# Two multiplication levels for items 0 and 1 too, with the weights' quarters formed in item 0 and the last convolution's banks named by number

## The chip, the core and the metric

The kernel runs on one core of a Trainium2 chip. The core has a matrix engine (TensorE, PE in the profile), a vector engine (VectorE, DVE), an activation engine (ScalarE, ACT), a general engine (GpSimd, POOL) and a queue engine that only issues transfers (SyncE, SP). Every engine runs its own instructions in the order in which they were written, and waits on others through semaphores. The metric is the device time of one whole execution in microseconds.

## The reference

Thirty-two items of 512 nodes and 512 features, in fp32, go through a masked attention layer with 8 heads of 64, a residual and a layer norm, and then through a graph convolution, a residual and a second layer norm:

```
q, k, v = x @ Wq + bq, x @ Wk + bk, x @ Wv + bv           # (32, 512, 512) each, split into 8 heads of 64
scores  = q k^T / 8 + where(adj == 0, -1e9, 0)            # (32, 8, 512, 512)
y       = softmax(scores) v
x1      = layernorm(x + y)
norm_adj = adj * rsqrt(deg)[:, None] * rsqrt(deg)[None, :],   deg = adj.sum(axis=1)
out     = layernorm(x1 + norm_adj @ (x1 @ W1) + b1)
```

`adj` is one 512x512 matrix for all items.

## The kernel before

**Projections by fewer products.** A 512x512x512 product (keys, queries, values, or the convolution's second factor) is cut into 2x2 blocks of 256 and computed with seven block products in place of eight; the price is sums and differences of blocks beforehand. The four such sums of a weight are `weigh_part` (line 228), those of `x` are `combine` (174). In one level each of the seven products (the table `CHAIN`, or `PLAIN_FIRST`, line 349, for item 0, whose operands come in another order) is four 128x256 matmuls. In two levels four of the eight matmul groups are taken into quarters: `LEAF` (367) is seven steps of four 128x128 matmuls on 128-wide quarters, and `OUTER` (368) three further products of the first level, four 128x256 matmuls each. Two levels need quarters of the operands too: `quarter` (179) forms those of `x` and `weigh_quarter` (272) those of a weight, both on POOL. A tile of a weight therefore has ten slots: four blocks, three sums, three of quarters. The fourth quarter sum goes back into one of the blocks, so that a weight with all four quarters can no longer be used in one level.

`seven` (374) walks such a table: a step multiplies into a PSUM bank of its region (A, B, D, M), and then `put` copies the bank to SBUF on ACT or `add` adds it on DVE. Where the next step accumulates into the same bank, or a later region takes over its number, PE has to wait until `put` or `add` has read it. `bank` hands out the eight PSUM banks in turn, or by `at=`.

Before, items 0 and 1 run in one level: `keys_and_queries` (458) makes a pair of key and query heads at once, and `values_of` (396) takes `PLAIN_FIRST` and `CHAIN`. From item 2 on `keys_or_queries` (481) and the second half of `values_of` run in two levels.

**The order of the work.** A loop over items (from about line 990) is laid out by hand. Item b does: scores and values products of head pairs 0 and 2 (`stretch`, 608, with `scores`, 535), the keys and queries of item b+1, scores and values products of pairs 1 and 3, then the convolution of item b-1 mixed with the values of item b+1. `play(main, beside)` writes the PE steps of `main` one by one, and after step n the work of the other engines given under key n in `beside`. Nothing is reordered after that: an engine meets its instructions exactly in this order, so a DVE instruction written ahead of another one delays it even if it is not urgent.

The work beside PE that the change touches:

- `accumulate` (552): POOL adds up the numerators `e` of a head pair over four node blocks into `acc`; `fold` (623): DVE turns and reduces `acc` to `folded`; `inverse_all` (684): PE spreads `folded` with one matmul, DVE takes the maximum with a tiny number and the reciprocal; `scale_head` (722): ACT scales one node block of one head with it (32 of these for an item).
- `turn` (143): DVE transposes an item's `x` in 32x32 blocks, two instructions an item. `turn_first` (151) does it for item 0's with PE.
- `adjacency` (314): PE transposes `adj` in 16 blocks, DVE makes the mask from the bank, ACT copies it twice. `degrees` (329) is a DVE reduction of 128x2048 and a few small operations; `compare` (323) is a DVE comparison and a DVE reduction over 128x512, done four times, for a flag that selects the general kernel if the inputs are out of the ordinary.
- `swap` (280): `Wq`'s and `Wv`'s sums share one tile, `wqv`, and are loaded into it in turn from DRAM, where they are stored (`stored`) in item 0.
- `load_residual` (198): four loads of an item's `x` rows, and a gather that adds the bias row.
- `block` (807): the convolution of the last item, in four PSUM banks; `extend`: POOL additions of the last but one.

In item 0 (from line 959) the values come first, then the weights' sums, then keys and queries for head pairs by twos with the adjacency beside them. In the loop's pass b = 0 the keys and queries of item 1 are computed with `fold`, `degrees`, `compare` and the sums of `W1` beside them, and the values of item 1 with folds, turns and the fourth quarters of `Wv` beside them.

Of the kernel before, what the change touches and what calls it, by code (L numbers as in the profile page):

```python
# [10 lines left out]
F32 = mybir.dt.float32  # L11
# [4 lines left out]
ALU = mybir.AluOpType  # L16
# [34 lines left out]
def unshifted(  # L51
# [57 lines left out]
    def run(pieces):  # L109
        for f in pieces:  # L110
            f()
# [67 lines left out]
    def quarter(at):  # L179
        old, new = XT[:, 1:5].rearrange("p k u (t o) -> p k u t o", t=2), QUARTERS  # L180
        to, a, c = (
            (new[:, 0], old[:, :, 0, 1], old[:, :, 0, 0]), (new[:, 1], old[:, :, 1, 1], new[:, 0]),
            (new[:, 2], old[:, :, 1, 1], old[:, :, 0, 1]), (old[:, :, 0, 1], old[:, :, 1, 0], new[:, 1]),
        )[at]
        gpsimd.tensor_tensor(to, a, c, ALU.subtract)
# [62 lines left out]
    wv = NUM[:, :4].rearrange("p e k (u o) -> p (e k) u o", u=2)  # L248
# [18 lines left out]
    wk_quarters, wqv_quarters = quarters_in(wk), quarters_in(wqv)  # L267
# [4 lines left out]
    def weigh_quarter(w, new, at, engine, last=None):  # L272
# [3 lines left out]
            (new[:, 2], old[:, :, 0, 0], old[:, :, 0, 1], ALU.subtract), (old[:, :, 0, 1] if last is None else last, old[:, :, 1, 0], new[:, 1], ALU.subtract),  # L276
        )[at]
        engine.tensor_tensor(to, a, c, op)

    def swap(k, slots=10):  # L280
        sync.dma_start(wqv[:, :slots], stored[k][:, :slots])
# [32 lines left out]
    def adjacency(k):  # L314
        for m in (2 * k, 2 * k + 1):
            p = bank([P, N])
# [79 lines left out]
    def values_of(b):  # L396
# [21 lines left out]
        if b < 2:  # L418
            return seven(CHAIN if b else PLAIN_FIRST, multiply, put, add)
# [37 lines left out]

    def keys_and_queries(b, r):
        def multiply(p, i, j, fresh):
            for c, w in enumerate((wk, wqv)):  # L460
                for u in range(2):
                    tensor.matmul(
                        p[:, c, :], w[:, i, u, ts(r, P)], XT[:, j, u, :],
                        start=fresh and c == 0 and u == 0, stop=u == 1, skip_group_check=True,
                    )

        def out(i, j):
            begin_kq(b)
            return KQ[b, r + 2 * i][:, :, ts(j, HALF)]

        def put(q, p):
            g = r + 2 * q[0]
            for c in range(2):
                scalar.activation(out(*q)[:, c], p[:, c], AF.Identity, bias=bias[:, c, g : g + 1], scale=1.0)

        def add(q, p):
            vector.tensor_add(out(*q), out(*q), p)

        return seven(CHAIN if b else PLAIN_FIRST, multiply, put, add)

    def keys_or_queries(b, c):
# [45 lines left out]
        inner, outer = (({"A": 2, "D": 3, "B": 0}, {"A": 4}), ({"A": 5, "D": 3, "B": 0}, {"A": 2}))[c]  # L527
        leaf = seven(LEAF, multiply_quarters, put, add, (4, P), places=inner)
        return leaf, [spread_last], seven(OUTER, multiply, None, add_outer, places=outer)

# [265 lines left out]
    def convolve(b):  # L796
# [10 lines left out]
        def block(m):  # L807
            if m == 0:
                t["p"] = [bank([P, N]) for _ in range(DT)]
# [157 lines left out]
    run(v[1:5])  # L967
    scalar.activation(wqv[:, :4], wqv[:, :4], AF.Copy, scale=SCALE)
    weigh(wk, gpsimd)
    run(v[5:])  # L970
    biases()
    wq_parts = each(lambda k: weigh_part(wqv, vector, k), *range(4))
    kq = keys_and_queries(0, 0)
    run(wq_parts[:2] + kq[:1] + wq_parts[2:3] + kq[1:2] + wq_parts[3:] + kq[2:])
    gather(first_rows, rows(bv))
    for w, new in ((wqv, wqv_quarters), (wk, wk_quarters)):
        for at in range(3):
            weigh_quarter(w, new, at, gpsimd)
    nc.sync.dma_start(stored[1][:, :7], NUM[:, :4].rearrange("p e k (u o) -> p (e k) u o", u=2)[:, :7])
    nc.sync.dma_start(stored[0], wqv)  # L980
    play(keys_and_queries(0, 1), {
        1: [lambda: adjacency(0)], 3: [lambda: turn(1, 0), lambda: adjacency(1)], 5: [lambda: turn(1, 1)],
    })
    for k in range(4):
        combine(1, k)
# [4 lines left out]
    for b in range(B):  # L990
# [31 lines left out]
        if b < LAST:  # L1022
            if b == 0:
                k0, k1 = keys_and_queries(1, 0), keys_and_queries(1, 1)
                main = [p for pair in zip(k0, k1) for p in pair]
                ahead_x = acts.tile([P, 2, 2, N], F32, name="x2", tag="lo", bufs=1)
                for j in range(2):
# [4 lines left out]
                    1: fold0, 2: [degrees], 3: weights[:1], 4: fold1, 5: weights[1:2] + exact[:1], 6: exact[1:2],  # L1032
                    7: weights[2:3], 8: exact[2:3], 9: weights[3:], 10: exact[3:],
                    12: each(lambda k: weigh_quarter(w1, w1_quarters, k, gpsimd), *range(3)),
                }
            else:
                (k_leaf, k_spread, k_outer), (q_leaf, q_spread, q_outer) = (keys_or_queries(b + 1, i) for i in range(2))
                main = (
                    k_leaf[:6] + k_outer[:1] + k_leaf[6:] + k_outer[1:2] + q_leaf[:6] + q_outer[:1] + q_leaf[6:]
                    + q_outer[1:2] + k_outer[2:3] + q_outer[2:3] + k_outer[3:] + q_outer[3:]  # L1040
                )
# [6 lines left out]
                    1: root + checks[:1], 2: checks[1:3], 3: checks[3:], 4: more[:1] if b > 1 else [],  # L1048
# [22 lines left out]
        elif b < LAST:  # L1071
            swap(1)
# [373 lines left out]
```

## Time and profile before

| What | Value |
| --- | --- |
| median of 3 timed runs | 2690.14 us (2690.1 to 2690.21) |
| the profiled execution's own time | 2690.48 us |
| span in its profile | 2688.5 us |
| PE busy | 2661.7 us (99%) |
| POOL, DVE, ACT busy | 2218.5 (83%), 2083.5 (77%), 1501.3 (56%) us |
| mean granted TensorE clock | 0.997 |
| keys and queries of item 0 / 1 / 3 | 22.70 to 48.72 / 63.00 to 87.37 / 23.22 us long |
| values of item 1 | 101.46 to 113.97 |
| convolution and values in a later item | about 31.0 us |

The profile names instructions by engine, operation and tile, `out<-in`; `xT` is the turned `x` with its block sums, `wk` and `wqv` the weights, `mm` a PSUM bank of a projection or of the convolution, `sc` one of scores, `av` one of values products, `kq` keys and queries, `e` the numerators. A fp32 matmul mostly leaves two records. All instructions show the line of one helper, L45, so they are told apart by tile. In a row of the timeline the first number is the start in microseconds, the second the length; a bracket at the end gives idle time before it and what ended it.

### The profile page before, as it was taken

To read this page: it belongs to the slowest core of one execution; us is meant where nothing else is said; L and a number is where in the kernel's file an instruction comes from. 1 tells how busy PE (TensorE), PEld (TensorE's weight loads), DVE (VectorE), ACT (ScalarE), POOL (GpSimd) and SP (SyncE) were. 2 spreads that over 40 slices of the span, in tenths; PEclk is the share of its full clock that TensorE was granted. 3 is DMA by queue.
4 is the path that set the end of the run, shared out by engine and by line. 5 is a ranking of instruction groups with operands and counts; after the bars stand their busy time and mean duration, and the time that the engine had idled before them with its cause. 6 is when DMAs were issued, how large, how long until landed. Compare 5 with 4: busy or idle time off the path is not lost.

```text
span 2688.5 us, 42635 instructions
## 1 busy us (share of the span) xinstructions
PE 2661.7 (99%) x15396; PEld 1935.9 (72%) x15396; DVE 2083.5 (77%) x3043; ACT 1501.3 (56%) x2677; POOL 2218.5 (83%) x1690
## 2 busy tenths in 40 slices
PE   9999999999999999999999999999999999999997
PEld 7677676776776866767767777677677677776765
DVE  4778877778778787787887787877878877778777
ACT  4456555565555565555655555555556555565554
POOL 5788888888898888888888888888888888888865
PEclk9999999999999999999999999999999999999999
DMA  6445446545455454455454554544555546545541
GB/s 196 148 109 160 137 115 165 150 124 144 132 149 150 125 155 142 119 156 142 142 140 119 166 149 119 156 137 131 153 129 158 138 117 166 153 118 148 148 97 53
DMA packets 422683, 373.30 MB, mean 139 GB/s; under 512 B 279872, under 2 KB 348992, under 8 KB 414272
## 3 DMA queue, kind: packets, MB, share of 16 engines
q1 hardware_dynamic: 388720, 304.16, 34.5%
q0 software_dynamic: 32736, 65.02, 15.7%
q8 instruction: 124, 2.03, 0.3%
q10 hardware_dynamic: 1008, 1.31, 0.1%
q14 instruction: 95, 0.78, 0.1%
HBM read 295.96 MB, written 41.16 MB: 125 GB/s over the span
## 4 chain that ended last, share of the span: by engine, by line
PE 96%; DVE 2%; POOL 1%; DMA 0%; ACT 0%; issue 0%; SPq 0%; POOLq 0%; DVEq 0%; ACTq 0%
PE mm L45 63%; PE sc L45 17%; PE av L45 16%; POOL acc L45 1%; DMA yT<-yb 0%; DVE st L45 0%; ACT yT L45 0%; DVE e L45 0%; SPq L45 0%; DVE folded L45 0%; DVE yT L45 0%; DMA xr<-in_x_dram 0%; DVE wk L45 0%; DVE yb L45 0%; DVE kq L45 0%
## 5 line engine op out<-in xcount | busy, mean ns | idle before, releaser
L45 POOL TENSOR_TENSOR acc<-acc,e 128x1024 f32<-128x1024 f32 x244 | 595.4, 2440 | 14.5
L45 DVE SCALAR_TENSOR_TENSOR e<-sc,maskT 128x1024 f32<-128x1024 f32 x512 | 585.2, 1216 | 21.3 <-PE sc L45 21.3
L45 ACT ACTIVATE e<-e 128x1024 f32<-128x1024 f32 x512 | 540.1, 1057 | 85.7 <-DVE e L45 55.4
L45 PE MATMUL sc<-kq 64*128 64x512 f32 x2048 | 456.9, 596 | 0.0
L45 PE MATMUL av<-e,v 128*64 128x512 f32 x2048 | 453.6, 595 | 0.3
L45 PE MATMUL mm<-xT,wk 128*128 128x256 f32 (+1 forms) x2512 | 393.3, 312 | 0.3 <-DVE kq L45 0.3
L45 POOL TENSOR_TENSOR xT<-xT 128x512 f32<-128x512 f32 x246 | 326.9, 1335 | 76.0 <-DVE xT L45 41.8
L45 PE MATMUL mm<-xT,wqv 128*128 128x256 f32 (+1 forms) x2512 | 387.9, 310 | 0.0
L45 PEld LDWEIGHTS mm<-xT,wk 128*128 128x128 f32 x2512 | 347.5, 191 | 46.7 <-DVE st L45 23.5
L45 PE MATMUL mm<-wqv,xT 128*128 128x128 f32 (+1 forms) x2456 | 379.0, 310 | 0.2 <-DVE v L45 0.2
L45 PEld LDWEIGHTS mm<-xT,wqv 128*128 128x128 f32 x2512 | 349.7, 191 | 21.3
L45 PEld LDWEIGHTS av<-e,v 128*64 128x64 f32 x2048 | 147.7, 137 | 298.9 <-issue 231.3
L45 POOL TENSOR_TENSOR e<-e 128x512 f32<-128x512 f32 x240 | 305.1, 1282 | 69.6 <-ACT e L45 54.5
L45 PEld LDWEIGHTS sc<-kq 64*128 64x128 f32 x2048 | 192.5, 187 | 232.5 <-issue 176.7
L45 PEld LDWEIGHTS mm<-wqv,xT 128*128 128x128 f32 x2456 | 343.7, 193 | 21.9 <-issue 0.8
L45 POOL TENSOR_TENSOR acc<-e 128x1024 f32<-128x1024 f32 x124 | 293.7, 2369 | 34.4 <-ACT e L45 34.4
L45 PE MATMUL mm<-w,e 128*128 128x128 f32 (+1 forms) x1680 | 297.9, 324 | 0.0
L45 ACT COPY kq<-mm 128x512 f32<-128x512 f32 x240 | 140.1, 584 | 256.2 <-PE mm L45 255.7
L45 PEld LDWEIGHTS mm<-w,e 128*128 128x128 f32 x1680 | 253.6, 191 | 24.8 <-DVE y L45 7.1
L45 DVE TENSOR_TENSOR v<-v,mm 128x512 f32<-128x512 f32 x217 | 146.2, 686 | 149.7 <-ACT v L45 76.3
L45 DVE SCALAR_TENSOR_TENSOR kq<-mm,bias,kq 128x256 f32<-128x256 f32 x420 | 183.7, 478 | 87.2 <-PE mm L45 49.8
L45 ACT ACTIVATE yT<-yT,inv 128x64 f32<-128x64 f32 x992 | 246.6, 337 | 0.0
(155 smaller groups left out, 3520.7 us busy)
## 6 DMA issues: line engine op xcount, KB each, us to landing
wqv<-wq_parts SPq DMA_DIRECT2D x30, 2560.0 KB, 11.7
wqv<-wv_parts SPq DMA_DIRECT2D x30, 2560.0 KB, 13.7
yT<-yb SPq DMA_DIRECT2D x508, 64.0 KB, 2.4
xr<-in_L_gnn_bv_dram POOLq DMA_DIRECT2D x31, 1024.0 KB, 11.2
xr<-in_x_dram SPq DMA_DIRECT2D x122, 256.0 KB, 4.2
e<-in_x_dram SPq DMA_DIRECT2D x240, 128.0 KB, 2.8
yT<-in_L_gnn_bias_dram POOLq DMA_DIRECT2D x30, 1024.0 KB, 16.5
out_dram<-y SPq DMA_DIRECT2D x116, 256.0 KB, 2.2
```

Source lines behind the costliest of these rows:

```text
L45: return self.tc.keep_in_program_order(op(*args, **kwargs))
```

## The change

Items 0 and 1 take two levels as well (item 0's values stay in one). `keys_and_queries` is gone; `projections` lists the steps of keys and queries in the order that item 2's had, and item 0 uses banks that differ in the leaf steps and in the regions of the outer ones. All four quarters of `Wk`, `Wv` and `Wq` are formed on POOL in item 0, and `Wv` and `Wq` are stored whole, so `swap` loads all ten slots each time and the patches of single slots in items 0 and 1 go. The quarters of item 0's `x` are formed on DVE. `adjacency` has its banks by number (6 and 7). In the pass b = 0 the four `compare` move from the keys and queries to the values of item 1, and behind them in DVE's order stand both `turn`s; the inverse of item 0 comes after the fifth leaf step. In the pass b = 1 the inverse comes two steps earlier, as in all later items, with the head scalings spread as there. In item 30 the residual load moves from step 8 to step 0 of the keys and queries. The last convolution's four banks are 0, 1, 3 and 5, and its tail does one addition fewer before its copies.

```diff
-    def quarter(at):
+    def quarter(at, engine=gpsimd):
...
-        gpsimd.tensor_tensor(to, a, c, ALU.subtract)
+        engine.tensor_tensor(to, a, c, ALU.subtract)
...
-    wv = NUM[:, :4].rearrange("p e k (u o) -> p (e k) u o", u=2)
+    wv = NUM[:, :5].rearrange("p e k (u o) -> p (e k) u o", u=2)
...
+    def weigh_quarters(w, new):
+        for at in range(4):
+            weigh_quarter(w, new, at)
+
+    def swap(k):
+        sync.dma_start(wqv, stored[k])
...
     def adjacency(k):
         for m in (2 * k, 2 * k + 1):
-            p = bank([P, N])
+            p = bank([P, N], at=6 + m % 2)
...
-        if b < 2:
-            return seven(CHAIN if b else PLAIN_FIRST, multiply, put, add)
+        if b == 0:
+            return seven(PLAIN_FIRST, multiply, put, add)
...
-        inner, outer = (({"A": 2, "D": 3, "B": 0}, {"A": 4}), ({"A": 5, "D": 3, "B": 0}, {"A": 2}))[c]
+        inner, outer = (
+            (({"A": 2, "D": 3, "B": 0}, {"A": 4}), ({"A": 5, "D": 3, "B": 0}, {"A": 2})) if b
+            else (({"A": 1, "D": 3, "B": 5}, {"A": 4}), ({"A": 0, "D": 3, "B": 5}, {"A": 2}))
+        )[c]
...
+    def projections(b):
+        (k_leaf, k_spread, k_outer), (q_leaf, q_spread, q_outer) = (keys_or_queries(b, c) for c in range(2))
+        main = (
+            k_leaf[:6] + k_outer[:1] + k_leaf[6:] + k_outer[1:2] + q_leaf[:6] + q_outer[:1] + q_leaf[6:]
+            + q_outer[1:2] + k_outer[2:3] + q_outer[2:3] + k_outer[3:] + q_outer[3:]
+        )
+        return main, k_spread, q_spread
...
-                t["p"] = [bank([P, N]) for _ in range(DT)]
+                t["p"] = [bank([P, N], at=k) for k in (0, 1, 3, 5)]
+                psum["n"] += 4
...
+    for k in range(3):
+        quarter(k, vector)
     scalar.activation(wqv[:, :4], wqv[:, :4], AF.Copy, scale=SCALE)
     weigh(wk, gpsimd)
+    weigh_quarters(wk, wk_quarters)
     run(v[5:])
+    quarter(3, vector)
     biases()
+    weigh_quarters(wv, wv_quarters)
+    nc.sync.dma_start(stored[1], wv)
     wq_parts = each(lambda k: weigh_part(wqv, vector, k), *range(4))
-    kq = keys_and_queries(0, 0)
...
-    for w, new in ((wqv, wqv_quarters), (wk, wk_quarters)):
-        for at in range(3):
-            weigh_quarter(w, new, at, gpsimd)
...
-    play(keys_and_queries(0, 1), {
-        1: [lambda: adjacency(0)], 3: [lambda: turn(1, 0), lambda: adjacency(1)], 5: [lambda: turn(1, 1)],
+    main, k_spread, q_spread = projections(0)
+
+    def store_parts():
+        weigh_quarters(wqv, wqv_quarters)
+        nc.sync.dma_start(stored[0], wqv)
+
+    play(main, {
+        0: wq_parts[:1], 1: wq_parts[1:2], 2: wq_parts[2:3], 3: wq_parts[3:] + [store_parts], 5: [lambda: adjacency(0)],
+        8: k_spread + [lambda: gather(first_rows, rows(bv))], 11: [lambda: adjacency(1)], 16: q_spread + [lambda: turn(1, 1)],
+        17: [lambda: turn(1, 0)], 18: [lambda: combine(1, 0)], 19: [lambda: combine(1, 1)],
     })
-    for k in range(4):
-        combine(1, k)
+    combine(1, 2)
+    combine(1, 3)
+    quarters()
...
             if b == 0:
-                k0, k1 = keys_and_queries(1, 0), keys_and_queries(1, 1)
-                main = [p for pair in zip(k0, k1) for p in pair]
...
-                    1: fold0, 2: [degrees], 3: weights[:1], 4: fold1, 5: weights[1:2] + exact[:1], 6: exact[1:2],
-                    7: weights[2:3], 8: exact[2:3], 9: weights[3:], 10: exact[3:],
-                    12: each(lambda k: weigh_quarter(w1, w1_quarters, k, gpsimd), *range(3)),
+                    2: fold0, 3: [degrees], 8: k_spread, 9: fold1 + weights[:2], 11: weights[2:], 16: q_spread,
+                    18: each(lambda k: weigh_quarter(w1, w1_quarters, k), *range(3)),
...
-                    5: first[:1] + ahead["root"] + store[:1], 6: store[1:3], 7: store[3:], 8: k_spread + load,
+                    0: load, 1: root + checks[:1], 2: checks[1:3], 3: checks[3:], 4: more[:1] if b > 1 else [],
+                    5: first[:1] + ahead["root"] + store[:1], 6: store[1:3], 7: store[3:], 8: k_spread,
...
-        if b == 0:
-            weigh_quarter(wqv, wqv_quarters, 3, gpsimd)
-            sync.dma_start(stored[0][:, 1:5, 0, P:], wqv[:, 1:5, 0, P:])
-            swap(1, 7)
-        elif b < LAST:
+        if b < LAST:
             swap(1)
...
-                play(values_of(1), {
-                    0: fold0, 1: fold1 + [weigh_values], 4: turn0, 5: end["inverse"],
-                    6: turn1 + combined + end["scale_heads"][24:] + end["scale_heads"][:8] + [lambda: swap(0)],
+                leaf, spread_last, outer = values_of(1)
+                heads = end["scale_heads"]
+                play(leaf[:6] + outer[:1] + leaf[6:] + [spread_last] + outer[1:], {
+                    0: fold0, 1: fold1 + [lambda: weigh_quarter(w1, w1_quarters, 3)], 4: end["inverse"],
+                    5: exact[:2] + heads[24:], 6: exact[2:] + heads[:8], 8: turn1 + turn0, 9: combined[:1], 10: combined[1:2],
+                    11: combined[2:] + [lambda: swap(0)],
                 })
...
-                        5: (end["inverse"] if b > 1 else []) + [lambda b=b: biased.extend(load_residual(b))],
-                        7: heads[:14] if b > 1 else end["inverse"], 11: heads[14:23] if b > 1 else heads[:23], 13: conv["open"] + ahead["judge"], 16: turn0,
+                        5: end["inverse"] + [lambda b=b: biased.extend(load_residual(b))], 7: heads[:14], 11: heads[14:23], 13: conv["open"] + ahead["judge"], 16: turn0,
...
-    run(extend[:3] + e["unload"] + e["parts"] + extend[3:] + end["grow"])
+    run(extend[:2] + e["unload"] + e["parts"] + extend[2:] + end["grow"])
```

## The prediction, made before the changed kernel ran

> **What bounds the kernel now.** I read the page first (busy shares, then the chain that ended last by engine), then that chain in order of time for the first items, then the timeline of each engine in the stretches that the diff touches.
>
> The busy shares and the chain by engine:
>
> ```profile
> span 2688.5 us, 42635 instructions
> PE 2661.7 (99%) x15396; PEld 1935.9 (72%) x15396; DVE 2083.5 (77%) x3043; ACT 1501.3 (56%) x2677; POOL 2218.5 (83%) x1690
> PE 96%; DVE 2%; POOL 1%; DMA 0%; ACT 0%; issue 0%; SPq 0%; POOLq 0%; DVEq 0%; ACTq 0%
> ```
>
> TensorE (PE) is the bound nearly everywhere: work taken from it is time won, and every hole in it is time lost. Next the chain in order of time, with the pieces of items 0 to 2 (start, length, what):
>
> ```profile
> 63.07 24.37 PE mm L45 x112
> ...
> 101.53 12.51 PE mm L45 x58
> ...
> 214.27 23.22 PE mm L45 x160
> ```
>
> Item 1's keys and queries in one level take 24.37 us (112 records, two to a matmul), its values 12.51 us; item 3's keys and queries, already in two levels, 23.22 us. So two levels are worth 1.15 us for a pair of keys and queries. Now the timeline, with the other engines' work around PE in items 0 and 1:
>
> ```profile
> 49.15 5.20 POOL L45 TENSOR_TENSOR xT<-xT 128x512 f32<-128x512 f32 x4 [13.66 <-DVE xT L45]
> 54.33 2.36 POOL L45 TENSOR_TENSOR acc<-e 128x1024 f32<-128x1024 f32 x1
> ...
> 66.92 1.22 DVE L45 TENSOR_REDUCE folded<-acc 128x32 f32<-128x1024 f32 x1
> 68.05 2.28 DVE L45 TENSOR_REDUCE deg<-yT 128x4 f32<-128x2048 f32 x1
> ...
> 82.97 0.69 DVE L45 TENSOR_TENSOR plainT<-plainT,adjT 128x512 f32<-128x512 f32 x1
> 83.69 0.69 DVE L45 TENSOR_REDUCE fine<-plainT 128x1 f32<-128x512 f32 x1
> ...
> 101.75 4.79 POOL L45 TENSOR_TENSOR acc<-acc,e 128x1024 f32<-128x1024 f32 x2
> ...
> 107.86 1.22 DVE L45 TENSOR_REDUCE folded<-acc 128x32 f32<-128x1024 f32 x1
> ...
> 111.93 0.39 PE L45 MATMUL mm<-folded,spread 128*128 128x128 f32 x2
> ```
>
> The reader is to see that in item 1's values PE reaches the `folded` matmul at 111.93, 2.9 us after DVE's last fold ended at 109.0: long values hid the folds. Last, what a hole costs besides itself. Item 31's values wait for a fold (timeline, then the stretches table, whose column 1.00 or 0.54 ahead of the DMA share is the granted clock):
>
> ```profile
> 2573.59 0.77 PE L45 MATMUL mm<-folded,spread 128*128 128x128 f32 x2 [3.79 <-DVE folded L45]
> 2574.15 8.94 PE L45 MATMUL mm<-wqv,xT 128*128 128x128 f32 x48
> ```
>
> ```profile
> 2574.00:2580.00 6.00, 6.00 (x32) 6.00 (x32) 2.29 (x7) 2.19 (x9) 0.00 (x0) 0.54 0.61 190
> ```
>
> After 3.79 us of idling the granted clock is 0.54, and the 48 records that follow take 8.94 us where the same ones of item 3 (at 260.92) take 6.40: 2.5 us more.
>
> **The change part by part.** Times below are on the profiled execution's clock.
>
> Units. A 128x256 matmul of `mm` issues every 0.4325 us (four in 1.73 us: 230.42 to 232.15 for the eight records of one step), a two-level leaf step of four 128x128 matmuls takes 0.90 us (258.92 to 260.70 for two). A projection in one level is 28 x 0.4325 = 12.11 us; in two levels 7 x 0.90 + 12 x 0.4325 = 11.49 us. Five projections change. DVE: an add from PSUM 0.62 apart, a bias-and-add on 256 columns 0.44, a turn 1.2. POOL: 128x512 1.30. ACT: a 512-column copy 0.48 apart.
>
> *1. Item 0's keys and queries* (22.70 to 48.72 before, with 1.74 us of adjacency transposes). PE's work falls by 1.1 us. New waits, in PE's order. POOL now runs the four weights' sums, then four quarters each of `wk`, `wv`, `wqv`: from 15.81 that is 26.2, 31.4 and 36.6. The keys' fifth step wants the fourth quarter of `wk` at 26.3: just in time. The queries' second and fifth steps want theirs at 32.5 and 36.3: 0.4 us of waiting in all. The second pair of adjacency banks stands in the middle of the queries' leaf: DVE masks (0.65 each) after its add, until 36.7, ACT then copies four times and only at 38.6 puts the block that the seventh accumulation follows; PE would be there at 37.55: 1.1 us. Then item 1's two turns stand on DVE between the outer products' adds, which PE must await before it accumulates again: 0.5 and 0.4 us. So 2.4 us of waiting against 1.1 won: scores start at 50.0 instead of 48.72. The score stage itself was stretched by DVE to 7.26 us and then takes its 7.0: the values matmuls start at 57.0 instead of 55.98, **+1.0 us**. Bounds: -1.1 (every wait covered) and +2.5 (DVE and POOL each a tenth slower). SP issues no more than before here; the stores of `wv` and `wq` are 3.4 us later or larger by 0.8 MB, and the scores' first `e` waits for the `wv` store: issued at 34.1 as before, its 1.8 MB landed in 6.8 us, 2.6 MB would land by 44, needed at 51.
>
> *2. Item 1's keys and queries* (63.00 to 87.37 before). POOL first adds the queries' side block (1.45 us, from 51.6), then item 1's remaining sums and four quarters: six operations, 53.0 to 60.8, where it formerly had done at 54.3. The first head pair's sums (three x 2.4) then end at 68.0 instead of 61.55. DVE's order is: keys' first add, fold (2.4), degrees (2.28 + 0.6), then the keys' next two adds. From 68.0 that ends at 74.6. PE, from 64.0, has done six leaf steps and one outer product by 71.2, and its last leaf step overwrites the bank that the second of these adds reads: it starts at 74.65. A hole of 3.4 us that was not there, against 1.15 won; the second fold and the weights' quarters on POOL lie beside the queries. This stage ends at 90.5, **+2.1 us** more (total 3.1). Bounds: -1.1 (no hole) and +4.
>
> *3. Item 1's values* (101.46 to 113.97 before; now from 104.6, 14.1 after the keys and queries as before). The swap of `wqv` is whole now, 2.5 MB; such swaps take 11.7 to 13.7 us to land (page, part 6), so it is in at 104.2 at the latest: covered by the scores and values matmuls, with 0.4 us to spare. The work falls by 0.6. The `folded` matmul comes after five leaf steps, at 109.1, but the folds end, as before, 21.6 us after the scores' start (POOL's two accumulations set it): 112.1. A hole of 3.1 us. Then DVE's queue, in the built order:
>
> ```
> v add x2 | inv x4, reciprocal | v add | (plainT equal, reduce) x4 | xT turn x2 | v add (outer 0,0) | ...
> ```
>
> from 112.1: 1.25, 1.25, 0.65 to 115.25; compares 4 x (0.69 + 0.69) = 5.5 to 120.75; turns 2.4 to 123.15; the add 0.65 to 123.8. The compares' rows run from 0.69 to 1.28 us for the first half, the slow ones beside a busy POOL; POOL idles here, so I take the row at 82.97 (with the slow rows 1.1 us more). PE finishes its last leaf step at 116.2, and its next product accumulates on the bank that this last add reads. It waits from 116.2 to 123.85: **7.6 us**. The two outer products that are left follow each other on one bank, so the second waits 0.85 for DVE. Without a slower clock they end at 128.2. A hole of 7.6 us is twice that of item 31, so its 2.5 us come on top: 130.8. Before, the next scores started at 113.97: +16.8 in all, **+13.7 us** of it here. Bounds of this part: +9 (the add somehow 2.5 us earlier and the clock kept) and +16. ACT's 16 head scalings (3.93 us from 114.6) and POOL's spread add lie inside the hole.
>
> [...]
>
> *4. Item 2's keys, queries, values.* POOL's last residual add for item 1 comes 0.45 us earlier against PE; the 0.28 us that PE waited at 136.01 go: **-0.3**. In item 2's values `inverse` moves two leaf steps ahead; its wait (0.59 before, at 177.81) grows by 1.8, since POOL's sums set it. The two waits of 0.99 and 1.04 after it were for DVE and for ACT's 23 head scalings; with 14 of these done earlier the second goes: **+0.8**. Bounds -0.5 and +2.
>
> *5. The tail.* With its banks by number the last convolution no longer waits 0.89 us for ACT's copy (at 2654.56): **-0.9**, bounds -1.5 and 0. The reordered extension stands on POOL beside matmuls; a POOL part that comes 1.3 us earlier can at most win within these bounds. In item 30 four loads go ahead of four stores on SP: 2 us later stores, for which nobody waits. Cost 0.
>
> Sum: 1.0 + 2.1 + 13.7 - 0.3 + 0.8 - 0.9 = **+16.4 us**. The profiled execution took 2690.48 us (span 2688.5), 0.34 over the median of the timed runs; 2690.14 + 16.4 = 2706.5 us, 0.6% slower.
>
> **The rivals.**
>
> *Only the short holes.* If DVE reached the outer add in time (compares and turns elsewhere than the order says), the 7.6 and 2.5 us go: +6.3, 2696.4 us. The built order speaks against it.
>
> *The gain goes through.* PE's work falls by 2 x 1.15 + 0.6 = 2.9 us, the tail by 0.9, and every new wait is covered: 2686.3 us, within 0.2%. For it: in items from 2 on the same form runs with hardly a hole. Against it: there a convolution's first 7.3 us lie between the attention and the values, and no degrees or compares stand on DVE.
>
> *The other side: item 30.* Its residual load goes eight steps ahead. If those loads are what slowed the `yT` pieces, which took 13.4 us to issue at 2557.95 against 8.1 elsewhere, PE's hole of 3.79 and the 2.5 us of slow clock go with it: 6.3 us. That decides only if the holes in item 1 sum to less than 4 us instead of 14; then 2680 us. Against it: the loads were issued at 2533.30, took 3.7 us, and were long in; the two POOL gathers issued at 2544.92 and 2545.79 (16.7 and 21.0 us to landing) stay where they are.
>
> *Worse.* The two 3 us holes cool the clock too: +2.5 each, 2711.5 us.
>
> **How the numbers follow.** Forecast 0.76, only short holes 0.08, worse 0.09, gain goes through 0.04, item 30 0.03. Range 2699 to 2712: the forecast with the bounds of parts 1 to 3 not all on one side, and the worse case. A measurement of this kernel tells about 0.2% (5.4 us) from no change: faster 0.03, same 0.04, slower 0.93.
>
> **What would show it.** In the profile after: PE idle for some 7 to 8 us in item 1's values, ended by DVE, with a granted clock near 0.5 behind it; a PE wait of some 3 us on DVE in item 1's keys and one on `folded` before the large one; the scores of item 1 near 131 instead of 114; all later items with the same 7.1, 7.0, 23.2 and 31.0 us. Scores at 114 to 118, or a hole that ACT or POOL ends, would prove me wrong.

## The result: 28.5 us slower, and where they are

The changed kernel takes 2718.6 us (median of 5 runs, 2716.6 to 2720.92) against 2690.14 us (5 runs, 2688.32 to 2691.3). The ratio is 1.0107, 95% interval 1.0092 to 1.0121. The direction was forecast; the size, 16.4 us, was not, and the time lies above the range of 2699 to 2712 us. The profiled execution is the slowest of the five, 2720.92 us with a span of 2719.0, so that the table below adds up to 30.5 us and not to 28.5.

The page of the changed kernel, its span, busy shares and the chain by engine:

```profile
span 2719.0 us, 42916 instructions
PE 2669.2 (98%) x15516; PEld 1939.7 (71%) x15516; DVE 2105.6 (77%) x3077; ACT 1499.3 (55%) x2665; POOL 2234.9 (82%) x1707
PE 93%; DVE 3%; POOL 2%; DMA 1%; issue 1%; SPq 0%; ACT 0%; ACTq 0%; POOLq 0%; DVEq 0%
```

PE's share of the chain falls from 96 to 93%; DVE's rises from 2 to 3%, POOL's from 1 to 2%. Laid side by side by the starts of PE's stages (the values products between them take 7.0 us in both):

| Stage (us) | before | after | difference | forecast |
| --- | --- | --- | --- | --- |
| up to the first keys and queries | 22.70 | 24.80 | +2.1 | 0 |
| item 0's keys and queries, first scores | 33.28 | 37.05 | +3.8 | +1.0 |
| item 1's keys and queries | 24.37 | 31.52 | +7.15 | +2.1 |
| item 1's values, next scores | 19.79 | 34.20 | +14.4 | +13.7 |
| item 2's keys and queries | 23.74 | 24.27 | +0.5 | -0.3 |
| item 2's convolution and values | 34.02 | 35.82 | +1.8 | +0.8 |
| item 2's scores to item 31's second scores | 2423.20 | 2424.26 | +1.1 | 0 |
| from there to the end | 65.19 | 64.86 | -0.3 | -0.9 |

PE's timeline in item 1 (start, length, tiles, shape; the bracket is the idle time ahead, called a hole below, and what ended it):

```profile
68.87 7.46 PE L45 MATMUL mm<-xT,wk 128*128 128x128 f32 x56
81.65 2.05 PE L45 MATMUL mm<-xT,wk 128*128 128x128 f32 x8 [5.32 <-DVE kq L45]
83.49 10.06 PE L45 MATMUL mm<-xT,wqv 128*128 128x128 f32 x64
...
114.48 4.73 PE L45 MATMUL mm<-wqv,xT 128*128 128x128 f32 x40
122.12 0.80 PE L45 MATMUL mm<-folded,spread 128*128 128x128 f32 x2 [2.91 <-DVE folded L45]
122.71 4.76 PE L45 MATMUL mm<-wqv,xT 128*128 128x128 f32 x24
134.37 3.78 PE L45 MATMUL mm<-wqv,xT 128*128 128x256 f32 x8 [6.90 <-DVE v L45]
139.01 1.99 PE L45 MATMUL mm<-wqv,xT 128*128 128x256 f32 x8 [0.85 <-DVE v L45]
```

The holes stand where the forecast had put them, 5.32, 2.91 and 6.90 us against 3.4, 3.1 and 7.6. The clock behind the first of them is the part that it had left out. The 64 records of the queries take 10.06 us here and 8.19 in item 2, and the eight ahead of them 2.05 instead of 1.13. The table of stretches, with the granted clock ahead of the DMA share (0.71, 0.50):

```profile
84.00:90.00 6.00, 6.00 (x41) 6.00 (x41) 3.54 (x4) 2.08 (x4) 5.45 (x5) 0.71 0.00 0
...
132.00:138.00 6.00, 3.63 (x8) 2.53 (x8) 2.32 (x3) 0.00 (x0) 1.26 (x1) 0.50 0.00 0
```

DVE and POOL ahead of the hole of 5.32 us:

```profile
72.81 2.36 POOL L45 TENSOR_TENSOR acc<-e 128x1024 f32<-128x1024 f32 x1
72.88 1.25 DVE L45 STREAM_TRANSPOSE acc<-acc 128x1024 f32<-128x1024 f32 x1 [0.27 <-POOL acc L45]
...
75.25 4.76 POOL L45 TENSOR_TENSOR acc<-acc,e 128x1024 f32<-128x1024 f32 x2
75.29 2.28 DVE L45 TENSOR_REDUCE deg<-yT 128x4 f32<-128x2048 f32 x1
...
77.81 2.23 DVE L45 TENSOR_SCALAR eps<-safe 128x4 f32<-128x4 f32 x1
...
80.22 1.28 DVE L45 TENSOR_TENSOR kq<-kq,mm 128x512 f32<-128x512 f32 x2
```

A four-column operation, `eps`, took 2.23 us and ended at 80.04, as POOL's sum beside it did (80.01). In the kernel before it did not fall beside one of POOL's long sums:

```profile
70.57 0.17 DVE L45 TENSOR_SCALAR eps<-safe 128x4 f32<-128x4 f32 x1
```

In item 0 POOL's sums and quarters of the keys' weight, DVE's sums for the queries' weight and PE's wait for the fourth quarter:

```profile
16.77 13.06 POOL L45 TENSOR_TENSOR wk<-wk 128x512 f32<-128x512 f32 x8
...
28.03 2.35 DVE L45 TENSOR_TENSOR wqv<-wqv 128x512 f32<-128x512 f32 x2
...
29.88 2.05 PE L45 MATMUL mm<-xT,wk 128*128 128x128 f32 x16 [1.35 <-POOL wk L45]
```

In item 2's values the inverse, two steps earlier than before, makes a hole of 2.39 us, and behind it the granted clock was 0.50 (208 to 210 us; the last row is the same work in item 3 of the kernel before):

```profile
205.79 0.46 PE L45 MATMUL mm<-folded,spread 128*128 128x128 f32 x2 [2.39 <-DVE folded L45]
206.09 7.98 PE L45 MATMUL mm<-wqv,xT 128*128 128x128 f32 x48
...
260.92 6.40 PE L45 MATMUL mm<-wqv,xT 128*128 128x128 f32 x48
```

That operations of DVE and of POOL took longer beside each other (`eps` 2.23 us for 0.17, POOL's eight in item 0 1.63 us each for 1.30) is what the forecast had not seen, and the runs below were made around it.

### The profile page after: what moved, and what is told of

It is laid out like the page before. It is cut to its first block, busy times and chain, and to the rows that moved or that the text cites. A ratio compares the mean times of both kernels' runs of the same rounds, so it can differ in the third digit from the quotient of the medians.

```text
span 2719.0 us, 42916 instructions
## 1 busy us (share of the span) xinstructions
PE 2669.2 (98%) x15516; PEld 1939.7 (71%) x15516; DVE 2105.6 (77%) x3077; ACT 1499.3 (55%) x2665; POOL 2234.9 (82%) x1707
## 3 DMA queue, kind: packets, MB, share of 16 engines
q8 instruction: 125, 2.05, 0.3%
## 4 chain that ended last, share of the span: by engine, by line
PE 93%; DVE 3%; POOL 2%; DMA 1%; issue 1%; SPq 0%; ACT 0%; ACTq 0%; POOLq 0%; DVEq 0%
PE mm L45 61%; PE sc L45 16%; PE av L45 16%; POOL acc L45 1%; DVE st L45 0%; DVE kq L45 0%; DMA yT<-yb 0%; DMA xr<-in_x_dram 0%; POOL xT L45 0%; DVE folded L45 0%; DVE low L45 0%; SPq L222 0%; DVE v L45 0%; DMA w<-in_L_gnn_weight_dram 0%; DVE yT L45 0%
## 5 line engine op out<-in xcount | busy, mean ns | idle before, releaser
L45 PE MATMUL mm<-xT,wk 128*128 128x128 f32 (+1 forms) x2560 | 390.7, 309 | 7.9 <-DVE kq L45 6.6
L45 PE MATMUL mm<-xT,wqv 128*128 128x128 f32 (+1 forms) x2560 | 386.1, 308 | 2.0 <-ACT kq L45 1.0
L45 POOL TENSOR_TENSOR e<-e 128x512 f32<-128x512 f32 x244 | 311.0, 1285 | 71.1 <-ACT e L45 54.5
L45 ACT COPY kq<-mm 128x512 f32<-128x512 f32 x256 | 149.5, 585 | 287.9 <-PE mm L45 287.4
L45 DVE SCALAR_TENSOR_TENSOR kq<-mm,bias,kq 128x256 f32<-128x256 f32 x448 | 195.9, 478 | 97.4 <-PE mm L45 54.8
```

Source lines behind the costliest of these rows:

```text
L45: return self.tc.keep_in_program_order(op(*args, **kwargs))
```

## The experiments

Single edits move the total by less than the runs of one kernel scatter (3 to 8 us), so they are judged by the stage that they touch. Of a stage, the time from its first matmul to the next stage's is given.

### One edit each, in the changed kernel

**The compares earlier.**

```diff
-        stretch(b, two, ... else fold0 + fold1 if b else ())
+        stretch(b, two, ... else fold0 + fold1 if b else exact)
-                    5: exact[:2] + heads[24:], 6: exact[2:] + heads[:8], ...
+                    5: heads[24:], 6: heads[:8], ...
```

> The four compares leave DVE's queue in item 1's values and go behind the first values product of item 0's second pair of stretches, where DVE is nearly idle. Theory (DVE's queue order sets the hole of 6.9 us, the cold clock follows from it): the time from the start of item 1's values to the next scores falls from 26.45 us by 5.5 us of compares and about 2 us of slow clock, to 18.5 to 19.5; a hole of 1 to 1.5 us is left, set by the turns; total about 7.5 us less than the changed kernel, near 2711. Rival (the turns wait for the load of item 2's x, or the swap of the values' weights is late): 26.4 stays, total near 2718.6.

Item 1's values take 26.32 us and the total is 2722.77 us (2716.23 to 2724.26): nothing gained. The hole on DVE's add fell from 6.90 to 2.81 us (theory: 1 to 1.5), but the one before `folded` grew from 2.91 to 8.19. DVE and POOL in this run:

```profile
111.76 2.13 DVE L45 TENSOR_TENSOR plainT<-plainT,adjT 128x512 f32<-128x512 f32 x1
...
113.42 5.45 POOL L45 TENSOR_TENSOR acc<-acc,e 128x1024 f32<-128x1024 f32 x2
...
114.53 2.13 DVE L45 TENSOR_TENSOR plainT<-plainT,adjT 128x512 f32<-128x512 f32 x1
...
117.29 2.12 DVE L45 TENSOR_TENSOR plainT<-plainT,adjT 128x512 f32<-128x512 f32 x1
```

and the same operation in the changed kernel, where POOL is idle:

```profile
125.27 0.68 DVE L45 TENSOR_TENSOR plainT<-plainT,adjT 128x512 f32<-128x512 f32 x1
```

Beside POOL's sums a compare took 2.13 us for 0.68, three times as long, and the folds behind the compares came late: what was won at one hole was lost at the other. The stage's time is the rival's number, but not by the rival's cause: what is late is still DVE's queue.

**The degrees earlier.**

```diff
-            gap = late + back["measure"][:3] if back else ()
+            gap = late + back["measure"][:3] if back else [degrees]
-                    2: fold0, 3: [degrees], 8: k_spread, ...
+                    2: fold0, 8: k_spread, ...
```

> The degrees leave the keys of item 1 and go between the two values products of item 0's first stretch. Theory (DVE's queue: degrees of 2.3 us and small operations of 2.6 us stand ahead of the add that frees a bank): the hole of 5.32 us falls to about 0.4, the slow clock behind it (2.8 us) goes, keys and queries of item 1 take 23.5 to 24.3 us instead of 31.52; total about 7.5 us less, near 2711. Rival (POOL's late sums alone set the hole): not over 1 us less.

Item 1's keys and queries take 29.83 us instead of 31.52, and the values after them 27.42; the total is 2719.57 us (2717.03 to 2721.25). Neither number was met. DVE's timeline:

```profile
65.53 2.25 DVE L45 TENSOR_REDUCE deg<-yT 128x4 f32<-128x2048 f32 x1
67.81 1.92 DVE L45 TENSOR_SCALAR safe<-deg 128x4 f32<-128x4 f32 x1
69.77 0.17 DVE L45 TENSOR_SCALAR eps<-safe 128x4 f32<-128x4 f32 x1
69.85 2.33 DVE L45 TENSOR_SCALAR fine<-deg 128x4 f32<-128x4 f32 x1
72.21 2.26 DVE L45 SCALAR_TENSOR_TENSOR fine<-deg,fine 128x4 f32<-128x4 f32 x1
74.39 0.70 DVE L45 STREAM_TRANSPOSE yb<-av 128x512 f32<-128x512 f32 x1
```

POOL in the same stretch:

```profile
67.36 4.79 POOL L45 TENSOR_TENSOR acc<-acc,e 128x1024 f32<-128x1024 f32 x2
72.11 2.34 POOL L45 TENSOR_TENSOR acc<-e 128x1024 f32<-128x1024 f32 x1
```

Three operations of four columns cost 6.5 us. POOL went from one sum to the next, and each of the three ends where one of POOL's sums does (69.73, 72.18 and 74.47). The adds of the keys, behind them, were late again, and PE had a hole of 3.81 us.

**The inverse later.**

```diff
-                    ... 4: end["inverse"], 5: exact[:2] + heads[24:], 6: exact[2:] + heads[:8], ...
+                    ... 5: exact[:2], 6: exact[2:], 7: end["inverse"] + heads[24:] + heads[:8], ...
```

> The inverse of item 0 moves from the fifth to the eighth step of item 1's values, the head scalings with it. Theory (DVE's chain of folds, inverse, compares, turns and add sets the end, so the two holes are one): the hole before the folded matmul shrinks from 2.9 to under 0.5 us, the one on DVE grows by as much, the stage stays at 26.45 within 1 us, total near 2718. Rival (the holes add): 23.5 us, total near 2715.5.

Values and next scores together take 34.82 us against 34.20 (the values alone 27.62 against 26.45, a little more than the 1 us that theory allowed); total 2719.43 us (2718.68 to 2721.9). The wait before `folded` is gone (it came to stand at a leaf step, 2.04 us), and the other grew:

```profile
122.41 1.27 PE L45 MATMUL mm<-wqv,xT 128*128 128x128 f32 x8 [2.04 <-DVE v L45]
...
132.40 3.78 PE L45 MATMUL mm<-wqv,xT 128*128 128x256 f32 x8 [8.29 <-DVE v L45]
```

The two holes of this stage are one chain on DVE, from the second fold to the add that PE needs, and only what shortens that chain counts.

**The sums of the keys' weight on DVE.**

```diff
-    weigh(wk, gpsimd)
+    weigh(wk, vector)
```

> The four sums of the keys' weight are done by DVE (0.7 us each) in place of POOL (1.3 to 1.6 us). Theory (POOL's queue in item 0, slowed beside DVE to 1.63 us an operation, sets the first holes of the keys and queries): the hole of 1.35 us goes and the keys and queries of item 0 take 27.5 to 28.5 us instead of 29.98, total 1.5 to 2.5 us less. Rival (DVE becomes the late one): adds come later, 30 us or more.

The rival won: item 0's keys and queries take 33.24 us; total 2721.04 us (2719.97 to 2725.98). PE's wait of 1.35 us for POOL is gone, but DVE's sums for the queries fell beside POOL's quarters of the values' weight (0.67 us each in the kernel before, where POOL was idle):

```profile
26.02 6.30 POOL L45 TENSOR_TENSOR e<-e 128x512 f32<-128x512 f32 x4
26.07 3.45 DVE L45 TENSOR_TENSOR wqv<-wqv 128x512 f32<-128x512 f32 x2
...
30.04 2.83 DVE L45 TENSOR_TENSOR wqv<-wqv 128x512 f32<-128x512 f32 x2
...
34.12 2.08 PE L45 MATMUL mm<-xT,wk 128*128 128x128 f32 x8 [3.11 <-DVE kq L45]
```

### Testing the two engines against each other

**The compares left out.**

```diff
-                exact = each(compare, *range(NT))
+                vector.memset(FINE[:, B : B + NT], float(N))
+                exact = [lambda: None] * NT
```

> The four compares are left out; their counts are set to the value that they have for ordinary inputs, so only the flag's test of the adjacency is missing. Theory A (in item 1's values the compares, 6.1 us of DVE while POOL is idle, stand in the chain from the last fold to the add that PE waits for): the stage falls from 26.45 to 18 to 20 us, total 6.5 to 8.5 us less than the changed kernel, near 2711. Moving them earlier gave nothing only because there they ran beside POOL at 2.13 us each and held up the folds. Theory B (something else on DVE, such as the turns, sets the end): under 2 us less.

Item 1's values take 20.60 us instead of 26.45, so the compares were 5.85 us of that stage; a little more than theory A's 20 was left, with a hole of 2.81 us behind the turns. The total did not follow: 2717.89 us (2716.5 to 2721.8), 0.7 us less than the changed kernel and not 6.5 to 8.5. In this profile 3.2 us of the gain are lost again between item 2's scores and item 31's; with item 0's order changed as well (the last run below) the compares are worth 4.6 to 6.8 us of the total.

**Item 0: DVE's sums where POOL is idle.**

```diff
-    weigh(wk, gpsimd)
+    weigh(wk, vector)
-    weigh_quarters(wv, wv_quarters)
-    nc.sync.dma_start(stored[1], wv)
...
         weigh_quarters(wqv, wqv_quarters)
         nc.sync.dma_start(stored[0], wqv)
+        weigh_quarters(wv, wv_quarters)
+        nc.sync.dma_start(stored[1], wv)
```

> The sums of the keys' weight on DVE as in the run before, and POOL's quarters of the values' weight behind those of the queries' weight, so that POOL is idle while DVE forms the queries' sums. Theory A (DVE operations on SBUF and POOL's hold each other up: 1.4 to 1.7 us for a DVE sum of 0.67, 1.6 for a POOL sum of 1.3): DVE's four sums take 2.7 us again, the waits of 3.1 us on DVE and of 1.3 us on POOL go, keys and queries of item 0 take 27 to 28.5 us in place of 33.2 with the sums alone moved and 30 to 31 in the changed kernel; total 2 to 4 us less than the changed kernel. Theory B (the number of operations on each queue counts, not what runs beside): 32 us or more.

Item 0's keys and queries take 27.30 us. Against the run with the keys' sums on DVE only the order of POOL's work differs, by which POOL is idle while DVE forms the queries' sums (the bracket of its row names a load of `x`, the last that it waited for by the profile; DVE's sums had ended at 29.51):

```profile
26.18 1.40 DVE L45 TENSOR_TENSOR wqv<-wqv 128x512 f32<-128x512 f32 x2
...
28.10 1.41 DVE L45 TENSOR_TENSOR wqv<-wqv 128x512 f32<-128x512 f32 x2
...
29.64 5.21 POOL L45 TENSOR_TENSOR wqv<-wqv 128x512 f32<-128x512 f32 x4 [3.47 <-DMA e<-in_x_dram]
```

Two sums cost 1.40 us in place of 3.45, and the stage is 5.9 us shorter with the same operations on the same engines: the hole of 3.11 us ahead of the keys' last step is gone, and the matmuls behind it are 3.0 us faster (8 and 24 records took 2.08 and 4.86 us there; in the second profile of this order 8 and 24 such records take 1.06 and 2.84). Transfers are not what lengthens the sums: the first two here ran at 0.70 us each with a DMA share of 1.24 (26 to 28 us), the second two of the other run at 1.42 us with a share of 0.29 (30 to 34 us). Theory A holds, except that the total (2717.42 us, 2715.28 to 2721.86) hardly moved; see the repetition below.

**The folds later.**

```diff
-                    2: fold0, 3: [degrees], 8: k_spread, 9: fold1 + weights[:2], 11: weights[2:], 16: q_spread,
-                    18: each(lambda k: weigh_quarter(w1, w1_quarters, k), *range(3)),
+                    8: k_spread + fold0, 10: fold1, 12: [degrees], 16: q_spread + weights,
...
-                    ... 1: fold1 + [lambda: weigh_quarter(w1, w1_quarters, 3)], 4: end["inverse"],
+                    ... 1: fold1 + [lambda: weigh_quarters(w1, w1_quarters)], 4: end["inverse"],
```

> In the keys and queries of item 1 both folds and the degrees go behind the keys' leaf on DVE, the sums of W1 on POOL go behind the queries' last spread and its quarters into item 1's values. Theory A (POOL's numerator sums, late by the quarters formed first, hold the first fold, and the adds behind it hold PE): with nothing that waits for POOL ahead of the keys' adds the hole of 5.32 us and the slow clock go, 23.5 to 25 us in place of 31.5; total 6 to 7.5 us less. Theory B (the adds themselves or ACT's copies are late): 29 us or more.

29.64 us: the hole in the keys is gone, as theory A had it, and one of 3.56 us stands in the queries, where the folds and the degrees (some 8 us of DVE) now precede the adds. So the late folds did hold the keys, but the place that I gave them was no better, and the time is theory B's number without its cause. The values behind take 28.25 us instead of 26.45; total 2720.39 us (2718.7 to 2721.8).

**The kernel before with the change's tail alone.**

```diff
-                t["p"] = [bank([P, N]) for _ in range(DT)]
+                t["p"] = [bank([P, N], at=k) for k in (0, 1, 3, 5)]
...
-    run(extend[:3] + e["unload"] + e["parts"] + extend[3:] + end["grow"])
+    run(extend[:2] + e["unload"] + e["parts"] + extend[2:] + end["grow"])
...
-                    5: ..., 8: k_spread + load,
+                    0: load, ..., 8: k_spread,
```

> The kernel before with only the change's tail: banks 0, 1, 3, 5 for the last convolution, the extension's order, and item 30's residual load eight steps earlier. Theory A (the wait of 0.89 us for ACT goes, a smaller one on DVE's sums of the last convolution comes): from item 31's last values product to the end 0.3 to 0.9 us less, total 0 to 1 us less than before. Theory B (the earlier load ends the hole of 3.79 us in item 31's values): 3 us or more less.

2692.84 us (2689.89 to 2701.37, 10 runs), ratio 1.0007 (0.9997 to 1.0017): no measurable effect. PE's timeline:

```profile
2574.92 0.46 PE L45 MATMUL mm<-folded,spread 128*128 128x128 f32 x2 [3.87 <-DVE folded L45]
2575.22 7.98 PE L45 MATMUL mm<-wqv,xT 128*128 128x128 f32 x48
...
2661.91 10.20 PE L45 MATMUL mm<-w,xT 128*128 128x256 f32 x46 [0.56 <-DVE xT L45]
```

The wait of 0.89 us for ACT is gone and 0.56 us for DVE have come; from item 31's last values product to the end the profile is some 0.4 us shorter, as theory A had it. The earlier load did not shorten the hole in item 31 (3.87 us, before 3.79), so the rival that rested on it falls.

### The same work elsewhere

**All moved.** Item 0 as above; the degrees' reduction between the first values products; the rest of it and the compares late in item 1's keys and queries; the second fold and the inverse late in item 1's values; the turns behind the add; item 1's inverse as before.

```diff
+                    5: fold0, 8: k_spread + fold1, 12: [degrees], 16: q_spread + exact[:1], 17: exact[1:2], 18: exact[2:3], 19: exact[3:],
...
+                    1: fold0 + weights + [lambda: sync.dma_start(stored[2], w1), lambda: weigh_quarters(w1, w1_quarters)], 6: fold1,
+                    9: end["inverse"] + heads[24:], 10: turn1 + heads[:8], 11: turn0 + combined + [lambda: swap(0)],
```

> The changed kernel with the same products on TensorE and the same work of the other engines, but put elsewhere: item 0 as in the run that moved its sums; the degrees' reduction between the first values products, the rest of it, both folds and the compares behind the keys' leaf of item 1, where POOL is idle; W1's sums and quarters in item 1's values; there the second fold, the inverse and the turns behind the adds that TensorE waits for; item 1's inverse as before. Theory A (the loss is only waits on DVE and POOL that the new order made): keys and queries of item 0 take 27.3 us, those of item 1 24 to 26, item 1's values 13 to 15.5, item 2's convolution and values 34.0; the scores of item 2 start at 202 to 206 us instead of 229.9 (before: 200.1), total 2690 to 2697. Theory B (two levels cost DVE and POOL so much more work in items 0 and 1 that it shows wherever it stands): the scores of item 2 start after 212 us.

2707.51 us (2701.51 to 2708.56), ratio 1.0056 (1.0039 to 1.0073). Item 0's keys and queries take 27.53 us, item 1's 24.85, and item 2's convolution and values 34.01, as expected. But item 1's values take 23.02, and the scores of item 2 start at 213.92, which is theory B's number. The rows show another reason than theory B's, a mistake in the order:

```profile
108.25 5.20 POOL L45 TENSOR_TENSOR w<-w 128x512 f32<-128x512 f32 x4
...
119.29 1.26 POOL L45 TENSOR_TENSOR w<-w,w_quarters 128x512 f32<-128x512 f32 x1 [1.92 <-DMA w_parts<-w]
120.51 1.26 POOL L45 TENSOR_TENSOR v<-v 128x512 f32<-128x512 f32 x1
121.80 0.69 DVE L45 TENSOR_TENSOR v<-v,mm 128x512 f32<-128x512 f32 x1 [7.46 <-POOL v L45]
...
122.54 3.78 PE L45 MATMUL mm<-wqv,xT 128*128 128x256 f32 x8 [7.41 <-DVE v L45]
```

POOL's values spread stood behind all of W1's work and behind the store of W1.

**W1's work behind the spread.** The edit against the run before; the rest of the degrees, too, moves, behind three of the four compares.

```diff
-                    5: fold0, 8: k_spread + fold1, 12: [degrees], 16: q_spread + exact[:1], ..., 19: exact[3:],
+                    5: fold0, 8: k_spread + fold1 + weights, 16: q_spread + exact[:1], ..., 19: [degrees], 20: exact[3:],
...
-                    1: fold0 + weights + [lambda: sync.dma_start(stored[2], w1), lambda: weigh_quarters(w1, w1_quarters)], 6: fold1,
+                    1: fold0, 6: fold1, 9: end["inverse"] + heads[24:] + [lambda: weigh_quarters(w1, w1_quarters)],
```

> As the run before, but POOL's sums of W1 go back beside item 1's keys and queries (behind the keys' spread) and its quarters in item 1's values behind the values' spread, for which an add of DVE waits, and then TensorE. Theory A (the hole of 7.4 us in item 1's values was POOL's 9 us of W1 work and the wait for its store ahead of that spread): the hole goes, item 1's values take 13 to 15.5 us instead of 23.0, the scores of item 2 start at 204 to 207 us instead of 213.9, total 2692 to 2699. Theory B (the second fold or the turns on DVE set the end there): 19 us or more, total near 2705.

2697.54 us (2695.48 to 2699.23, 7 runs), ratio 1.0027 (1.0016 to 1.0038). Item 1's values take 14.72 us, with holes of 1.07 and 0.85 us left; the scores of item 2 start at 206.85 us, before at 200.11. These are theory A's numbers. With the same products on TensorE, 21 of the 28.5 us are gone, so theory B of the run before falls. What is left, 6.7 us by that start, is spread over the stages up to item 2's keys and queries, 2.2 us the largest piece; this order does not beat the kernel before.

### Once more, and two together

> The kernel with item 0's sums moved, a second time, for the holes of items 3 to 31, which took 8 us in its first profile and 1 us in that of the changed kernel. Theory A (they are fixed by the kernel): the same places, in items 3, 11, 13, 18 and 28, and 6 to 9 us in all again. Theory B (they fall by chance from run to run): other places or sizes, 1 to 5 us in all.

The same kernel as the one with item 0's order, profiled a second time: from item 2's scores to item 31's second scores 2423.76 us, the first time 2431.35, before 2423.20. So the 8 us of holes in items 3 to 28 belong to the first execution and not to the kernel, and that is where its gain had gone; theory A falls, and what is left, 0.6 us over before, is even less than theory B's 1 to 5. The time is now 2715.24 us (2714.08 and 2716.41).

> Both edits in one: item 0's sums moved and the compares left out (their counts set to the value for ordinary inputs, so the flag's test of the adjacency is missing). Theory A (the two losses are separate and add): the keys and queries of item 0 take 27.3 us, item 1's values 20.6, the scores of item 2 start at 217 to 219 us instead of 229.9; the total follows, less what the later items lose, 2706 to 2712. Theory B (a shorter front is lost again in the later items): the total stays at 2715 or more.

2710.63 us (2708.5 to 2712.3), 8.0 us less than the changed kernel; item 0's keys and queries 27.45 us, item 1's values 22.66, the scores of item 2 at 219.85. The two losses add nearly: from the first keys to item 2's scores the single edits win 3.8 and 4.2 us against the changed kernel, both together 7.4. The values' 2.1 us over the 20.6 expected are more than accounted for by two products that took 2.94 and 3.78 us here and 1.99 each there.

## Why the prediction was wrong

*Right: what happens in item 1's values.* The stage was forecast at 26.2 us and took 26.45. Its steps, the fold, the inverse, eight compare operations, two turns and the add ahead of PE, came in the forecast order. PE went on 19.9 us after the stage's start (forecast 19.25) and took 6.6 us from there (forecast 6.95), so the agreement is not one of large errors that cancel. The experiments show compares of 5.85 us in it, and that its two holes are one chain.

*Wrong: POOL and DVE were costed as if alone.* This is the step that failed first. Part 1 took 1.30 us for each of POOL's quarters, with the fourth of `wk` at 26.3, "just in time", and bounded the error at a tenth. The eight operations took 13.06 us, 1.63 each, beside DVE's quarters of `x` and its sums for the queries, and ended at 29.83. Those sums took 1.2 to 1.4 us instead of 0.67. Keys and queries took 30.0 us instead of the 27.3 that part 1 had worked out (30.2 to 31.5 in the five runs below that keep this order of item 0), and with the first scores the stage went up by 3.8 us instead of 1.0. With DVE's sums where POOL is idle it took 27.0 to 27.5 us in five runs; that this is part 1's number is in part luck, since that order is another one. In part 2 the late folds were right to the tenth of a microsecond (POOL's first three sums ended 18.0 us after the scores began, as forecast), but `eps` was taken at its old 0.17 us and took 2.23: the hole was 5.3 us and not 3.4.

The rows were there. In the profile of before three compares out of four took 0.86 to 1.28 us and one 0.69, and I named the slow ones "beside a busy POOL" without asking what else would come to stand beside POOL. In the runs compares took 0.68 us with POOL idle and 2.13 us beside its sums, and four-column operations 0.17 and up to 2.33, while adds that read PSUM stayed at 0.69 and block transposes at 1.25 in the same stretches (71.92 and 72.88 us of the changed kernel, beside POOL's sums of 2.4 us). What makes the two engines hold each other up no run here shows.

*Wrong: the clock behind the holes in item 1's keys and item 2's values.* Part 2 had no price for it; it was in the rival "worse", with 2.5 us. It cost 2.8 us (10.06 for 8.19 and 2.05 for 1.13). Together with the 2.1 us of `eps` this is nearly the whole 5 us by which that stage was short. Part 4, too, had no price for it, and there it cost 1.6 us: the wait for the inverse grew from 0.59 to 2.39 us as forecast, but the granted clock behind it fell to 0.50 (208 to 210 us), and the 48 records took 7.98 us for 6.40.

*Small.* Item 2's values: of the two later waits, 0.99 and 1.04 us before, 0.53 us is left, a little better than forecast; with the inverse moved back the stage took 34.01 us, as before. Item 2's keys: the wait of 0.28 us, which was to go, grew to 0.82 us. The tail gave 0.3 in place of 0.9, since a wait on DVE's last sums took its place. The 2.1 us at the start are a late landing of the first weights in this execution, for which PE waited 1.21 us until 8.83: other runs of the changed order start their keys and queries at 21.9 to 23.2 us. Only 0.7 to 1.7 us of it reach item 0's scores, which start at 53.1 to 54.1 us in the five runs with the same order of item 0 and at 54.78 here; the forecast was 50.0.

*Rivals.* "Only the short holes" and "the gain goes through" are excluded by the holes; the one that rested on item 30's load by the run of the tail alone. "Worse" priced the clock behind the short holes, and was still 7 us short, since it left POOL's and DVE's costs as they were.

*Open.* What makes the holes in the later items, 0 to 8 us in all in the profiles of the changed orders, was not settled. PE's brackets name DVE's folds and adds in most of them, and they differ between two executions of the same kernel. In one case the same overlap is seen: in item 28 two DVE operations of 32 columns took 0.84 and 1.20 us ahead of a hole of 1.64 us in the first execution of item 0's order, and 0.19 us each, with no such hole, in the second. Why POOL and DVE met there once and not the other time stays open.

## What to carry to other kernels

A product saved on the bounding engine is worth its time only if the others can deliver sooner: by the forecast's count 2.9 us of TensorE work were saved, and it was the stretch with the least cover, the first two items, that had to pay. Cost an operation of DVE and one of POOL by rows in which the other was busy, and ask of each moved operation what POOL does at that moment, not only what is queued ahead of it. When an edit empties one wait, look first at whether the next instruction of the same queue is late: two of the edits here (compares, inverse) moved a hole without shortening the stage, and two (degrees, folds) won under 2 us where some 7 were expected.

## What the runs showed that was not expected

- An operation of DVE on four columns took 0.17 us in the kernel before, and 1.92 to 2.33 us in the run with the degrees earlier, where POOL's 2.4 us sums follow each other.
- A hole's length alone did not say what it cost. In the profile of each of the two kernels, from 20 us to the last matmul, the granted clock changed only at moments that lie whole multiples of 3.41 us apart, wherever the holes stood: before, it fell to 0.50 at 2572.72 us and came back at 2579.54; in the changed kernel it fell to 0.50 at 80.60, 121.56, 131.80, 206.89 and 2606.46 us and came back at 87.42, 124.97, 138.62, 210.30 and 2609.87. In the 3.41 us ahead of each of the six falls PE had been idle for 2.31 to 3.41 us (2.31 us of 203.48 to 206.89, by the hole of 2.39 us); in the other such intervals at full clock it was never idle for more than 1.68 us.
- Behind holes of one length the same matmuls took different times. Ahead of `folded`, 2.91 us in the changed kernel put 2.35 us into one such interval, the clock fell to 0.50, and the 24 records behind it took 4.76 us; behind 2.91 us in the run with both edits they took 3.92. Behind 2.93 us they took 4.77 us in the run without the compares, and 3.91 in the second profile of item 0's order. The forecast had left the clock behind its holes of 3.1 and 3.4 us to a rival with a chance of 0.09. The hole in item 1's keys, grown to 5.3 us, held the whole of 77.18 to 80.60 us in the changed kernel, with the clock at 0.50 from 80.60.
